# Own part of layers three and four folded into the seven quarter products

## The chip, the cores and the metric

The kernel runs on one core of a Trainium2 chip. The metric is the device time of one execution in microseconds, the median of three runs. All tensors are fp32. TensorE multiplies into PSUM, VectorE (DVE), ScalarE (ACT) and GpSimd (POOL) work on SBUF, and the SyncE queue issues the transfers from and to HBM.

## The reference

There are 16 graphs (batches) of N = 1024 nodes with D = 128 features, each with its own adjacency matrix. Two graph networks follow one another, each with a residual and a layer norm:

```python
def _L0_gnn_ref(embeddings, adjacency_matrix, cost_matrix, W, b):
    degree = adjacency_matrix.sum(axis=-1)[:, :, None]
    sum_neighbors = jnp.einsum('bid,bij->bjd', embeddings, cost_matrix) / degree
    concatenated = jnp.concatenate([embeddings, sum_neighbors], axis=-1)
    return jax.nn.relu(jnp.einsum('bnk,dk->bnd', concatenated, W) + b)

def _layer(nodes, adj, ws, bs, wd, bd, wn, bn, wu, bu):
    src_agg = jnp.einsum('bjv,bij->biv', nodes @ ws + bs, _l2norm(adj, 2))
    dst_agg = jnp.einsum('bjv,bji->biv', nodes @ wd + bd, _l2norm(adj, 1))
    self_rep = nodes @ wn + bn
    upd = jnp.concatenate([src_agg, self_rep, dst_agg], axis=2)
    return jnp.tanh(upd @ wu + bu)
# four layers; inputs: x | layer 1 | layer 2 with layer 1 | layer 3 with layer 1 and x
x = _layernorm(x + _L0_gnn_ref(x, adj, adj, W, b))
x = _layernorm(x + _L1_gnn_ref(x, adj, ...))
```

The layers of the second network take 128, 128, 256 and 384 input features, that is 1, 1, 2 and 3 chunks of 128. `_l2norm` divides adj by the root of the sum of squares of its rows or columns.

## The kernel before, in words

The weights are multiplied through first: in each layer the kernel needs *message weights* (ws and wd times their parts of wu) and *own weights* (wn times its part of wu, the tiles `wown`). Features lie transposed, 128 features on the partitions and 1024 nodes in the free dimension.

A layer has two stages. `messages` (L595) multiplies features by message weights into PSUM, in four groups of nodes, and DVE adds the bias at L607, which gives the tiles t. Then DVE forms sums of quarters of t: S3 (L619, in two halves), S1 (L620), S2 (L621), S4 (L622). `aggregate` (L655) then adds three parts into the same sums: the messages times adj (DST), the messages times adj transposed (SRC), and the own part, which is own weights times features. For the first two, t and adj are cut in 2 x 2 quarters and multiplied in the Strassen-Winograd way: seven products M1, M2, M3, M4, Z11, Z12, Z21 of quarters and of sums of quarters instead of eight. The sums of adj's quarters are the tiles T2 to T4 and Q2 to Q4 (`combined`, `combine_1` and `combine`, L577 to L591). The results are put together afterwards by ACT copies and DVE additions (L685 to L715), and `squash` applies tanh.

Each product makes 64 rows, half of the 128 columns of the array. So the lists `upper` and `lower` name two streams of matmuls, one for each half of the array, and the loop at L765 issues one of each in turn: one step. `events` puts the reads of finished products, and `hooks` other work, ahead of a step of a given number. In before the own part stands first in both lists: for each chunk and each half of the nodes one matmul above and one below, so 2, 2, 4 and 6 steps in layers one to four. Every layer besides has 28 steps for messages (14 in each of DST and SRC). Batch 0 does its layer one in `plain_layer` (L625).

Every engine works its own list in the written order (`manual_schedule`, L794). What belongs to the next batch is hooked into the stages of the present one: in layer three the scaling of the next adj by its column norms (L345, after the transfer of cinv) and its first quarter sums, then directly `first_gnn` of the next batch (L470, records m_f and z_f, with L452, L461, L467 and L498 to L518 on DVE), and in layer four its layer norm: sum (L361), centring (L368), squares (L377, hook 0, the name v), then after a small matmul (pv) the line L385 (ve), a power on GpSimd (L387), and the scaling L392 (y). After that come the transposed features x1 (L427), T2 (L587) and T3 (L589), transposes of rows (L564), the end of the layer (L694, L711, L698, L702, L703, L775), and the next batch's layer one: L607, S3 and so on, more transposes, T4 (L591), and Q2 (L587) to Q4.

Message weights are kept in HBM (`wsave`) and loaded before each layer into one buffer, tag "wm" (`message_weights`, L172). Own weights stay in SBUF for the whole run (L99).

Of the kernel before, what the change touches and what calls it, by code (L numbers as in the profile page):

```python
# [23 lines left out]
def adj_resnorm_kernel(ctx: ExitStack, tc: tile.TileContext, x, adj, w0, b0, layers, out):  # L24
# [67 lines left out]

    ident = const.tile([P, P], F32, name="ident")
    fold = const.tile([P, P], F32, name="fold")
# [3 lines left out]
    b0c = const.tile([P, 1], F32, name="b0c")  # L98
    wown = [const.tile([P, CHUNKS[l], P], F32, name=f"wown{l}") for l in range(NL)]  # L99
    bout = [const.tile([P, 1], F32, name=f"bout{l}") for l in range(NL)]  # L100

    one = ctx.enter_context(tc.tile_pool(name="one", bufs=1))
    two = ctx.enter_context(tc.tile_pool(name="two", bufs=2))
    wsave = [kept_weights.tile([P, CHUNKS[l] + 1, 2 * P], F32, name=f"wsave{l}") for l in range(NL)]

# [19 lines left out]
    def fetch_weights(raw, l, q, wm=None):  # L125
        ws, bs, wd, bd, wn, bn, wu, bu = layers[l]
        nch = CHUNKS[l]
        flat = raw.take(max(3 * nch * P, (nch + 1) * 2 * P))
        wr = flat[:, :3 * nch * P].rearrange("p (k c v) -> p k c v", k=3, c=nch)
        for k, w in enumerate((ws, wd, wn)):  # L130
            q.dma_start(wr[:, k], w.rearrange("(c p) v -> p c v", p=P))
        wur = raw.take(3 * P).rearrange("p (k v) -> p k v", k=3)
        q.dma_start(wur, wu.rearrange("(c p) v -> p c v", p=P))
        bc = raw.take(4)
        for k, v in enumerate((bs, bd, bn, bu)):
            q.dma_start(bc[:, k:k + 1], v.rearrange("(p o) -> p o", o=1))
        if wm is None:
            wm = flat[:, :(nch + 1) * 2 * P].rearrange("p (c v) -> p c v", c=nch + 1)
        return wr, wur, bc, wm, [raw.take(3 * P).rearrange("p (k v) -> p k v", k=3) for _ in range(nch)]
# [21 lines left out]
    def fold_end(l, fetched):  # L161
        _, wur, _, wm, wTs = fetched
        for c in range(CHUNKS[l]):
            pm = small(f"wm{l}_{c}", [HW])
            for k in range(3):
                nc.tensor.matmul(pm[:, k * P:(k + 1) * P], wTs[c][:, k], wur[:, PART[k]],
                                 start=True, stop=True)
            nc.scalar.copy(wm[:, 1 + c], pm[:, :2 * P])
            nc.scalar.copy(wown[l][:, c], pm[:, 2 * P:3 * P])
        nc.sync.dma_start(wsave[l], wm[:, :CHUNKS[l] + 1])  # L170

    def message_weights(b, l):  # L172
        wm = message_tile(f"wm{l + 1}_{b}")
        nc.sync.dma_start(wm[:, :CHUNKS[l] + 1], wsave[l])
        return wm
# [294 lines left out]
    def first_gnn(b, msgs, xT, y, T2, dinv):  # L470
# [38 lines left out]

        events = {4: m1_and_m4_read, 8: m2_read, 10: m3_read}  # L510
        up, lo = flat_steps(upper, high), flat_steps(lower, low)
        for i, pair in enumerate(zip(up, lo)):
            if i in events:
                events[i]()
            for o, x_, y_, start, stop in pair:
                nc.tensor.matmul(o, x_, y_, start=start, stop=stop)  # L516
        nc.vector.tensor_add(e0, e0, Z0)
# [10 lines left out]
    def flat_steps(groups, rows):  # L528

        flat = []  # L530
        for m, (acc, first, mms) in enumerate(groups):
            later = [g[1] for g in groups[m + 1:] if g[0] is acc]
            last = not later or later[0]
            for i, (x_, y_) in enumerate(mms):
                flat.append((acc[rows], x_, y_, first and i == 0, last and i == len(mms) - 1))
        return flat

    def add_x(yT, xT, h):
# [85 lines left out]

    def plain_layer(b, l, feats, t, a, at, fT, etag, hooks):  # L625

        w = wown[l]
        Z = [product(f"z{h}_{l}_{b}", h) for h in range(NH)]  # L630
# [6 lines left out]

        steps = [(Z[h], w[:, c], blocks(f[:, half(h)]), k == 0, False) for h in (1, 0) for k, (f, c) in enumerate(feats)]
        steps += [(Dn[h], x(j, DST), a[:, j, half(h)], k == 0, k == NB - 1) for h in (1, 0) for k, j in enumerate(latter)]
# [14 lines left out]

    def aggregate(b, l, feats, msgs, a, at, T, Q, fT, etag, hooks={}, pieces=1):  # L655


        w = wown[l]
        n = len(feats)
        X, S = msgs  # L660
# [11 lines left out]

        def own(v, h):
            return [(w[:, c, v * V:(v + 1) * V], blocks(f[:, half(h)])) for f, c in feats]

# [25 lines left out]
        def second_half():  # L701
            nc.vector.tensor_add(e2, e2, Z1)  # L702
            nc.vector.tensor_add(e1, e1, e2)  # L703
# [14 lines left out]
        if l == 0:  # L718
# [16 lines left out]

            events = {8: m3_half, 12: m1_read, 20: m4_and_m2_read, 24: last_reads}
        else:

            first_of_lower = [(Ck, True, prod("M4", DST) + prod("M4", SRC)), (Dk, True, prod("M3", DST))]
            reads_of_lower = [m4_read, m3_half]  # L740
            if l < NL - 1:
                first_of_lower.reverse()
                reads_of_lower.reverse()
            upper = [
                (Z1, True, own(1, 1)), (Z0, True, own(1, 0)),
                (A, True, prod("M1", DST) + prod("M1", SRC)), (Bk, True, prod("M2", DST) + prod("M2", SRC)),
                (A, True, prod("M3", SRC)),
                *((Z0, False, prod("Z21", part)) for part in ((SRC, DST) if l == NL - 1 else (DST, SRC))),
            ]
            lower = [  # L750
                (Z1, True, own(0, 1)), (Z0, True, own(0, 0)),
                *first_of_lower,
                (Z1, False, prod("Z12", SRC) + prod("Z12", DST)),
# [3 lines left out]
            def first_reads():  # L757
                m1_read()
                reads_of_lower[0]()

            events = {8: first_reads, 12: reads_of_lower[1], 16: m2_and_half_of_m3, 20: last_reads}

        up, lo = flat_steps(upper, high), flat_steps(lower, low)
        assert len(up) == len(lo)
        for i, pair in enumerate(zip(up, lo)):  # L765
            if i - 2 * n in events:
                events[i - 2 * n]()
            if i in hooks:
                hooks[i]()
            for o, x, y, start, stop in pair:  # L770
                if len(y.shape) == 4:
                    o = nodes(o)
                nc.tensor.matmul(o, x, y, start=start, stop=stop)  # L773
        if pieces == 1:
# [15 lines left out]
    def feature(b, tag):  # L790
        return one.tile([P, N], F32, tag=tag, name=f"{tag}{b}")

    eng = mybir.EngineType
# [201 lines left out]
    for b in range(B):  # L995
# [8 lines left out]
        if b == 0:  # L1004
# [50 lines left out]
            T = combined(0, "T")  # L1055
            plain_layer(b, 0, feats, t, a, at, f1, "acc", hooks)
            wm = message_weights(b, 1)
            a2 = load(n)
            xs2 = load_spread(n)
        else:  # L1060
# [4 lines left out]
            t = messages(b, 0, feats, wm)  # L1065
            wm = message_weights(b, 1)
            Q = combined(b, "Q")

            def rows3():
# [10 lines left out]
            def first_addition(st=st):  # L1080
                if nxt:
                    add_squares(n, st, 1)

            hooks = {0: rows3, 3: lambda: combine(4, y, T), 5: lambda: combine_1(yt), 7: lambda: combine(2, yt, Q),
                     9: lambda: combine(3, yt, Q), 11: lambda: combine(4, yt, Q), 17: sums1, 28: first_addition}
            aggregate(b, 0, feats, t, a, at, T, Q, f1, "row", hooks)
            a2, xs2 = w.get("a"), None

# [3 lines left out]
        t = messages(b, 1, feats, wm)  # L1092
        wm = message_weights(b, 2)

# [18 lines left out]
        else:  # L1113
# [24 lines left out]
            hooks = {0: begin1, 11: centre1, 14: squares1, 18: rstd1, **sums_of_next}  # L1138
        aggregate(b, 1, feats, t, a, at, T, Q, f23, "row", hooks)
        if b:  # L1140
# [61 lines left out]
        t = messages(b, 2, feats, wm, between)  # L1202
        wm = message_weights(b, 3)
        aggregate(b, 2, feats, t, a, at, T, Q, f23, "acc", hooks)
        if nxt:
# [73 lines left out]
        else:  # L1279
            x1v = one.tile([P, HW], F32, tag="x", name="x1_last")  # L1280
            nc.scalar.copy(nodes(x1v), blocks(x1T[:, half(0)]))

            def residual_last():
                o = nodes(f4[:, half(1)])
                nc.vector.tensor_add(o, o, blocks(x1T[:, half(1)]))

            def transpose_last():
                pn["last"] = ps_t.tile([P, BPH, P], F32, tag="pt", name="on_1")
                for q in range(BPH):
                    i = BPH + q  # L1290
                    nc.tensor.transpose(pn["last"][:, q], f4[:, i * P:(i + 1) * P], ident)
                stats[1] = norm_stats(pn["last"], range(BPH), f"1_{b}_1", True)
# [3 lines left out]
        if nxt:  # L1296
            wm = message_weights(n, 0)
            T[4] = one.tile([P, NJ, HW], F32, tag="T4", name=f"T4_{b}_again")
        aggregate(b, 3, feats, t, a, at, T, Q, f4, "row", hooks, 1 if nxt else 2)
        if nxt:  # L1300
# [12 lines left out]
    for i in pieces:  # L1313
        pn[i] = ps_t.tile([P, 2, P], F32, tag="pt", name=f"on_0_{i}")
        for q in range(2):
            nc.tensor.matmul(pn[i][:, q], x1v[:, (i + q) * P:(i + q + 1) * P], ident, start=q == 0, stop=False)
    for q in range(BPH):
# [3 lines left out]
    for i in pieces:  # L1321
        for q in range(2):
            nc.tensor.matmul(pn[i][:, q], f4[:, (i + q) * P:(i + q + 1) * P], ident, start=False, stop=q == 1)
        stats[i] = norm_stats(pn[i], range(2), f"1_{b}_0_{i}")
# [33 lines left out]
```

## Time and profile before

| | |
|---|---|
| time, median of 3 (lowest to highest) | 2424.94 us (2424.76 to 2425.18) |
| span of the profiled execution | 2421.9 us |
| granted TensorE clock | full in nearly the whole span |
| layer three, `aggregate`, batch 3: 563.41 to 591.00 | TensorE 27.59 us busy, DVE 24.38 |
| layer four, batch 3: 616.81 to 646.22 | TensorE 29.41, DVE 22.31 |
| layer one, batch 4: 649.68 to 675.44 | TensorE 25.76, DVE 23.98 |
| layer two, batch 4: 678.93 to 705.00 | TensorE 26.07, DVE 22.62 |

A line of the timeline gives the start, the duration, the engine, the line of the kernel, the operation, what is written from what, the shape, and how many neighbours of one kind were joined; brackets tell the engine's idle time before it and who ended it. A line of the groups gives the same for all instructions of a kind, with busy time and the mean of one in ns. PEld is the loading of weights into the array, which goes on beside the matmuls. The ends of matmuls are modelled, so that durations of TensorE overlap; their starts are what counts.

### The profile page before, as it was taken

To read this page: it belongs to the slowest core of one execution; us is meant where nothing else is said; L and a number is where in the kernel's file an instruction comes from. 1 tells how busy PE (TensorE), PEld (TensorE's weight loads), DVE (VectorE), ACT (ScalarE), POOL (GpSimd) and SP (SyncE) were. 2 spreads that over 40 slices of the span, in tenths; PEclk is the share of its full clock that TensorE was granted. 3 is DMA by queue.
4 is the path that set the end of the run, shared out by engine and by line. 5 is a ranking of instruction groups with operands and counts; after the bars stand their busy time and mean duration, and the time that the engine had idled before them with its cause. 6 is when DMAs were issued, how large, how long until landed. Compare 5 with 4: busy or idle time off the path is not lost.

```text
span 2421.9 us, 34377 instructions
## 1 busy us (share of the span) xinstructions
PE 2407.9 (99%) x13245; PEld 955.6 (39%) x13245; DVE 1904.8 (79%) x2495; ACT 958.5 (40%) x1794; POOL 273.5 (11%) x100
## 2 busy tenths in 40 slices
PE   8999999999999999999999999999999999999998
PEld 5433343333433343333433434334333343333433
DVE  5878878798787978879788787887878878797743
ACT  5425334262442624435143352533425334262321
POOL 4100111101111011110011110111100111101100
PEclk9999999999999999999999999999999999999999
DMA  9517254261633517235172442725427264361410
GB/s 210 116 47 148 49 125 87 68 126 44 144 73 81 109 45 163 62 83 107 49 153 60 90 100 65 143 53 109 88 67 141 46 129 87 68 123 44 97 25 9
DMA packets 365731, 219.92 MB, mean 91 GB/s; under 512 B 152768, under 2 KB 336832, under 8 KB 365568
## 3 DMA queue, kind: packets, MB, share of 16 engines
q1 hardware_dynamic: 364800, 215.36, 42.0%
q0 software_dynamic: 768, 2.36, 0.3%
q8 instruction: 105, 1.72, 0.3%
q14 instruction: 58, 0.48, 0.1%
HBM read 199.17 MB, written 18.46 MB: 90 GB/s over the span
## 4 chain that ended last, share of the span: by engine, by line
PE 97%; DMA 1%; SPq 1%; DVE 0%; ACT 0%; issue 0%; POOLq 0%; DVEq 0%
PE m L773 44%; PE z L773 26%; PE pt L183 16%; PE m_f L516 5%; PE pw L183 2%; PE z_f L516 2%; DMA raw<-in_L_gnn_ws_dram 1%; PE z L652 1%; ACT Q L556 0%; SPq L549 0%; PE d L652 0%; DMA wsave<-wm 0%; DMA a<-in_adj_dram 0%; DMA raw<-in_L_gnn_wn_dram 0%; PE pv L183 0%
## 5 line engine op out<-in xcount | busy, mean ns | idle before, releaser
L773 PE MATMUL m<-Q,S 128*64 128x512 f32 x1008 | 444.9, 593 | 0.0
L387 POOL TENSOR_TENSOR rs<-ve,mhalf 128x32 f32<-128x32 f32 x30 | 191.6, 6385 | 1941.5 <-DVE ve L385 1941.5
L773 PE MATMUL m<-T,S 128*64 128x512 f32 x1008 | 394.9, 593 | 0.0
L773 PE MATMUL m<-at,t 128*64 128x512 f32 x1008 | 394.2, 593 | 0.0
L773 PE MATMUL m<-a,t 128*64 128x512 f32 x1008 | 391.7, 593 | 0.0
L607 DVE TENSOR_TENSOR t<-pt,wm 128x512 f32<-128x512 f32 x256 | 173.3, 686 | 138.4 <-PE pt L183 138.4
L773 PEld LDWEIGHTS m<-Q,S 128*64 128x64 f32 x1008 | 135.6, 137 | 280.1 <-issue 270.0
L686 ACT COPY e<-m 64x512 f32<-64x512 f32 x63 | 36.7, 582 | 501.8 <-PE m L773 501.4
L773 PE MATMUL z<-a,S 128*64 128x512 f32 x504 | 227.0, 593 | 0.0
L773 PE MATMUL z<-a,t 128*64 128x512 f32 x504 | 226.8, 592 | 0.0
L773 PE MATMUL z<-at,S 128*64 128x512 f32 x504 | 226.7, 592 | 0.0
L773 PE MATMUL z<-at,t 128*64 128x512 f32 x504 | 226.6, 592 | 0.0
L773 PE MATMUL z<-Q,t 128*64 128x512 f32 x504 | 226.6, 592 | 0.0
L183 PE MATMUL pt<-wm,f1T 128*64 128x256 f32 x1536 | 213.3, 381 | 0.0
L345 DVE TENSOR_TENSOR a<-a,cinv 128x512 f32<-128x512 f32 x250 | 154.3, 694 | 27.8 <-DMA cinv<-dr 22.3
L773 PEld LDWEIGHTS m<-T,S 128*64 128x64 f32 x1008 | 120.1, 137 | 137.1 <-issue 135.3
L773 PE MATMUL z<-T,t 128*64 128x512 f32 x384 | 172.8, 592 | 0.0
L773 PEld LDWEIGHTS m<-at,t 128*64 128x64 f32 x1008 | 117.9, 137 | 135.9 <-issue 131.6
L773 PEld LDWEIGHTS m<-a,t 128*64 128x64 f32 x1008 | 119.1, 137 | 129.6 <-issue 126.2
L183 PE MATMUL pt<-wm,f23T 128*64 128x256 f32 x1024 | 154.1, 379 | 0.0
L253 ACT ACTIVATE sq<-a 128x1024 f32<-128x1024 f32 x120 | 125.8, 1049 | 69.1 <-DVE acc L262 63.0
L183 PE MATMUL pt<-wm,x_T 128*64 128x256 f32 x1024 | 135.5, 379 | 0.0
(238 smaller groups left out, 4196.9 us busy)
## 6 DMA issues: line engine op xcount, KB each, us to landing
a<-in_adj_dram SPq DMA_DIRECT2D x120, 512.0 KB, 11.2
a<-in_adj_dram SPq DMA_DIRECT2D x240, 128.0 KB, 4.3
rows<-in_adj_dram SPq DMA_DIRECT2D x240, 64.0 KB, 3.0
wm<-wsave SPq DMA_DIRECT2D x16, 512.0 KB, 4.7
xn<-in_x_dram SPq DMA_DIRECT2D x124, 64.0 KB, 1.9
wm<-wsave SPq DMA_DIRECT2D x31, 256.0 KB, 3.9
xs<-in_x_dram SPq DMA_DIRECT2D x60, 128.0 KB, 3.6
cinv<-dr SPq DMA_DIRECT2D x30, 256.0 KB, 5.2
```

Source lines behind the costliest of these rows:

```text
L183: nc.tensor.matmul(out[s], x[:, s], y, start=start, stop=stop)
L253: nc.scalar.activation(sq, a[:, i, :], AF.Square, accum_out=state["cols"][:, i:i + 1])
L345: engine.tensor_mul(a[:, i, s], a[:, i, s], cinv[:, s])
L387: nc.gpsimd.tensor_tensor(rstd, ve, mhalf[:, :n], ALU.pow)
L516: nc.tensor.matmul(o, x_, y_, start=start, stop=stop)
L607: nc.vector.tensor_add(t[j][:, o:o + 2].rearrange("p k a v c -> p k (a v c)"), pt, wm[:, 0][:, None, :].to_broadcast([P, 2, 2 * P]))
L652: nc.tensor.matmul(nodes(o) if len(y.shape) == 4 else o, x_, y, start=start, stop=stop)
L686: nc.scalar.copy(e0[high], A[high])
L773: nc.tensor.matmul(o, x, y, start=start, stop=stop)
```

## The change

The own part of layers three and four is a product as well: own weights (128 outputs, 256 inputs) times features (256 inputs, 1024 nodes). With two chunks taken together it can be cut into quarters like the messages, and then its own seven products can be added into the sums of M1 to Z21 directly, as one more row of each. Layer three has just two chunks; in layer four two of its three are paired and the third (`rest`) stays as it was. This is meant to spare matmuls of TensorE.

For it the weights need quarter sums (`own_sums`, four small DVE operations once a layer, at the start) and the features need them in each batch (`feature_sums`, four DVE operations of 128 x 512, written over the features, in layer three partly into a buffer of tag "wm"). M3 is made in both halves of the array, a part in each; its own row is cut in two pieces of 256 nodes, so the two lists are no longer in step: `in_turn` orders the matmuls by the columns issued so far. Wider changes follow: the order of the products in layers three and four, and the numbers of events; own weights of layers one and two lie in the message tile and are loaded with it (so that tile's load for the next layer moves to a hook, 3 in layers one and two, 23 in layer three); the identity lies in the buffer of e0 and is made again for the end of the last batch.

```diff
+    PAIRED = {2: (1, 0), 3: (1, 2)}
+    wx = {l: const.tile([P, REST + (CHUNKS[l] - 2) * P], F32, name=f"wx{l}") for l in PAIRED}
+    ident = one.tile([P, HW], F32, tag="e0", name="ident")[:, :P]
...
+    def own_sums(l):
+        def w(at):
+            return wx[l][:, at:at + V]
+        nc.vector.tensor_sub(w(S3W), w(0), w(S1W))
+        nc.vector.tensor_add(w(S1W), w(S1W), w(P + V))
+        nc.vector.tensor_sub(w(S2W), w(S1W), w(0))
+        nc.vector.tensor_sub(w(S4W), w(P), w(S2W))
...
+    def in_turn(up, lo):
+        order, at = [], 0
+        for i, step in enumerate(up):
+            order.append((at, 0, i, step))
+            at += step[-1]
+        end, at = at, 0
+        for step in lo:
+            order.append((at, 1, None, step))
+            at += step[-1]
+        assert at == end
+        for _, _, i, step in sorted(order, key=lambda v: v[:2]):
+            yield i, step[:-1]
...
+            y4, y3 = (y[0, 1], y[0, 0]) if sums is None else sums
+            def feature_sums():
+                nc.vector.tensor_sub(y4, y[0, 1], y[0, 0])
+                nc.vector.tensor_sub(y[1, 1], y[1, 1], y4)
+                nc.vector.tensor_sub(y3, y[1, 1], y[0, 0])
+                nc.vector.tensor_sub(y[1, 0], y[1, 0], y[1, 1])
...
+            own_of = {"M1": (w(0), y[0, 0]), "M2": (w(S2W), y[1, 1]), "M3": (w(S3W), y3), "M4": (w(S1W), y4),
+                      "Z11": (w(P), y[1, 0]), "Z12": (w(S4W), y[1, 1]), "Z21": (w(P + V), y[1, 0])}
...
+            lower_m3 = of_own("M3", slice(0, G // 2)) + m3[NJ - 1:]
+            upper_m3 = m3s[:NJ - 1] + of_own("M3", slice(G // 2, G)) + m3s[NJ - 1:]
...
+            if l < NL - 1:
+                upper = [
+                    (A, True, of_own("M1") + prod("M1", DST) + prod("M1", SRC)),
+                    (Bk, True, prod("M2", DST) + prod("M2", SRC) + of_own("M2")), (A, True, upper_m3),
+                    (Z0, True, prod("Z21", DST) + prod("Z21", SRC) + of_own("Z21")),
+                ]
+                lower = [
+                    (Z1, True, of_own("Z12")), (Z0, True, of_own("Z11") + z11[:2]), (Dk, True, m3[:NJ - 1]),
+                    (Ck, True, m4), (Dk, False, lower_m3), (Z1, False, z12), (Z0, False, z11[2:]),
+                ]
+                events = {2: feature_sums, 9: m1_read, 16: m4_read, 18: m3_half_and_m2_read, 23: m3_read, 26: second_half}
+            else:
+                upper = [
+                    (Z1, True, own(1, 1, rest)), (Z0, True, own(1, 0, rest)),
+                    (A, True, of_own("M1") + prod("M1", DST) + prod("M1", SRC)),
+                    (Z0, False, of_own("Z21")),
+                    (Bk, True, of_own("M2") + prod("M2", DST) + prod("M2", SRC)), (A, True, upper_m3),
+                    (Z0, False, prod("Z21", SRC) + prod("Z21", DST)),
+                ]
+                lower = [
+                    (Z1, True, own(0, 1, rest)), (Z0, True, own(0, 0, rest)),
+                    (Z1, False, of_own("Z12")), (Z0, False, of_own("Z11")),
+                    (Ck, True, m4), (Dk, True, m3[:NJ - 1] + lower_m3),
+                    (Z1, False, z12), (Z0, False, prod("Z11", SRC) + prod("Z11", DST)),
+                ]
+                events = {4: feature_sums, 11: m1_read, 13: m4_read, 17: m3_half, 21: m2_and_half_of_m3, 26: last_reads}
...
+        sums = message_tile(f"fs_{b}").rearrange("p c v -> p (c v)")
+        hooks = alongside(hooks, {23: weights3})
-        aggregate(b, 2, feats, t, a, at, T, Q, f23, "acc", hooks)
+        aggregate(b, 2, feats, t, wm, a, at, T, Q, f23, "acc", hooks, sums=(sums[:, half(0)], sums[:, half(1)]))
```

In layer four hooks at the same number as an event come after it; `feature_sums` is event 4 there, `squares0` (L377) hook 0 and `rstd0` (L385 and L387) hook 7. In layer three `feature_sums` is event 2 and the next batch's hooks are 2 (L312), 4, 5, 7 and 9 (L345) and later.

## The prediction

> **What bounds the kernel now.** I read the shares of the engines first, then the groups by shape, the waits, and the timeline of batch 3 and the start of batch 4.
>
> ```profile
> PE 2407.9 (99%) x13245; PEld 955.6 (39%) x13245; DVE 1904.8 (79%) x2495; ACT 958.5 (40%) x1794; POOL 273.5 (11%) x100
> ...
> L773 PE MATMUL z<-f1T,wown 128*64 128x512 f32 x384 | 96.0, 592 | 0.0
> ...
> L183 PE MATMUL pt<-wm,f1T 128*64 128x256 f32 x1536 | 213.3, 381 | 0.0
> ```
>
> TensorE is never idle for long; VectorE (DVE) fills 79%. Each matmul of the program leaves two records, and two column halves run at once. In the timeline, pairs of 512-wide records start 0.43 us apart (664.27, 664.70, 665.13), so one step (an upper and a lower matmul of 512 columns) takes 2 x 0.427 = 0.855 us, 0.858 for the own part, and 256-wide ones half of that (four records in 0.43 us). The period of one batch is 148.5 us (L619 of layer one stands at 502.09 and again at 650.62), almost all of it such steps. But an average hides where DVE sets the pace. The layer-four stage of batch 3 runs from 616.9 to 646.2, then come the messages and layer one of the next batch:
>
> ```profile
> 621.61 1.21 DVE L377 TENSOR_REDUCE v<-sq 128x32 f32<-128x1024 f32 x1
> 623.24 0.19 DVE L385 TENSOR_SCALAR ve<-pv 128x32 f32<-128x32 f32 x1 [0.42 <-PE pv L183]
> 623.34 2.28 DVE L591 TENSOR_TENSOR T_again<-a,T 128x2048 f32<-128x2048 f32 x1
> 630.94 1.23 DVE L392 TENSOR_TENSOR y<-y,rs 128x1024 f32<-128x1024 f32 x1 [5.32 <-POOL inv L240]
> ...
> 647.01 0.65 DVE L775 TENSOR_TENSOR e<-e,z 128x512 f32<-128x512 f32 x1
> 647.59 1.28 DVE L607 TENSOR_TENSOR t<-pt,wm 128x512 f32<-128x512 f32 x2
> 649.03 0.69 DVE L607 TENSOR_TENSOR t<-pt,wm 128x512 f32<-128x512 f32 x1 [0.17 <-PE pt L183]
> 649.89 0.69 DVE L607 TENSOR_TENSOR t<-pt,wm 128x512 f32<-128x512 f32 x1 [0.17 <-PE pt L183]
> 650.62 0.76 DVE L619 TENSOR_TENSOR S<-t 128x256 f32<-128x256 f32 x2
> ```
>
> The numbers in brackets are DVE's idle time before the line. From 630.94 on there is next to none: one wait of 0.68 us for a copy of ScalarE, then 0.17 twice. From 650.62 to 665.03 there is none at all. And at the end of that run TensorE takes its operand as it is written:
>
> ```profile
> 662.74 2.29 DVE L587 TENSOR_TENSOR Q<-at 128x2048 f32<-128x2048 f32 x1
> ...
> 665.08 0.13 PEld L773 LDWEIGHTS m<-Q,S 128*64 128x64 f32 x1 [0.67 <-DVE Q L587]
> 665.09 0.13 PEld L773 LDWEIGHTS m<-at,t 128*64 128x64 f32 x1
> 665.13 0.60 PE L773 MATMUL m<-Q,S 128*64 128x512 f32 x1
> ```
>
> Q2 (L587) ends at 665.03, its weight load starts 0.05 us later, its matmul another 0.04 us later and 0.42 us after the one before it, so on its beat. The load had waited 0.67 us. Hence a DVE chain from L385 of layer four to Q2 of the next layer one meets TensorE with only some 0.02 us to spare, in every batch.
>
> [...] L392 waits 5.32 us for the power on GpSimd (L387, 7.34 us from 623.57) and nothing written after it moves ahead. So a sum put before L385 delays all that follows. [...] no stretch of before has the two column halves out of step, as the change makes them.
>
> **The change, part by part.** *Removed on TensorE.* The own part of layer three goes from 8 half-array matmuls (4 steps) to seven products, 3.5 steps; layer four from 6 steps to 2 + 3.5. That is 0.5 x 0.858 = 0.43 us for each layer and batch: 32 x 0.43 = 13.7 us at most.
>
> *Halves out of step.* The two 256-wide halves of M3 lie at different places, so the halves of the array run half a matmul apart for 5.5 steps in layer three and 8.5 in layer four. Not shown in the trace: between no cost (independent halves) and a whole slot of 0.43 us for each lone half, 2 x 0.43 a layer against the ideal 0.43 for the two together, which eats the gain. I take no cost, and keep 0.43 us a layer for the range.
>
> *Added on DVE.* Four chained operations (feature_sums) of 128x512 in each of the two layers. The nearest rows are L620 to L622 of the same shape and also chained: 0.69 us each, starts 0.725 apart. 32 x 4 x 0.69 = 88 us of DVE, hidden or not by place:
>
> In layer three they stand after L622 and before L312. For batches 1 to 14 DVE then waits 2.02 us for the DMA of cinv, which takes most of the 2.9; the scaling at L345 starts some 0.7 us later. That is worked off before L498 of the next batch's first network (first_gnn, which follows layer three directly), which sat idle 1.40 us. I cost it at nothing. The M1 product now needs the third message addition (done 563.89) at 564.27 and the fourth (564.48) at 565.98: met. TensorE gains its 0.43 us. In batch 0 the stage after it is already DVE-bound (the weights of x and e take 4.62 us there instead of 3.43): no gain.
>
> In layer four they stand between L377 and L385. Start 622.75, then 3 x 0.725 and one 0.61 to the next independent operation: L385 starts at 625.54 instead of 623.24, 2.30 us later (2.9 less the 0.42 that it waited for pv and the overlaps). Behind L385 stand the power on GpSimd, 7.34 us, and L392, which waits for it; the idle 5.32 us stays, since it follows L385. L392, the x1 transposes, T2, T3, the transposes of rows 2 and 3, and L775 all come 2.30 later. The four L607 then find their inputs ready and run 0.64 apart, from 649.89: the fourth at 651.81 instead of 649.89, S3 at 652.54 instead of 650.62. So 1.92 us remain. TensorE, 0.43 us early, stands at the first M3 of layer one at 650.97 and waits for S3 until about 653.04 (2.07 us); 16 steps later it wants Q2, at 666.73, and gets it at 665.03 + 1.92 + 0.08 = 667.03 (0.30 us more). Against 665.13 before that is 1.90 us later. The 0.43 us of layer four is used up in this wait.
>
> *Moved.* Own weights of layers one and two ride with the message weights: 64 KB more in each of 31 loads. The load for layer two landed at 673.35, needed at 675.4; it may come 2.3 + 0.3 later while its need comes 1.9 later: still met. The load for layer four now starts at hook 23 of layer three, and layer one of the next batch lies between. The four small own_sums fall into the start of batch 0, where DVE had idle stretches of 1.31 and 2.96 us. The identity in e0's buffer, and the copies of x1 and the second identity in the last batch, stand beside 10 us of layer-four messages on TensorE. Cost: nothing.
>
> *Sum.* Fifteen passages from layer four to the next batch at +1.90 = +28.5; layer three in batches 1 to 14, 14 x -0.43 = -6.0; batch 15, without a next one, both layers, -0.86. Together +21.6 on 2424.94: **2446.5 us**, forecast 2446.
>
> **The rivals.** *A: the sums hide, TensorE counts.* For it: TensorE is 99% busy and DVE has 20% idle, 5.32 us of it in this very stage. Then 31 x 0.43 = 13.3 us come off (batch 0's layer three gains nothing): 2411.6. Against: the idle time lies behind L385, which the sums precede, and Q2 has no slack. *B: the delay of DVE is half of what I take*, because some of the run from L392 to Q2 has slack that the line view does not show: 15 x 0.95 - 6.9 = +7, 2432; if it only balances the gain, no change. *C: as forecast, but lone halves cost their slot.* In layer four this drowns in the wait for S3; in layer three the gain goes, +6: 2453; another 0.43 a layer on top would make 2459. For it: no row shows it either way.
>
> **How the numbers follow.** Forecast 0.66, C 0.17, B 0.08 (a third of it within 0.2%), A 0.09. The range leaves out A and the low half of B, and C's worst end: 2435 to 2456. Faster by over 0.2%: A, 0.09. Within 0.2%: 0.03. Slower: 0.88.
>
> **What would show it.** Right: L385 starts about 2.3 us later, counted from the end of layer four's messages; TensorE shows a gap near 2 us before the first M3 of layer one in batches 1 to 15, a smaller one before Q2, and none in layers two to four; layer three lasts 27.15 us instead of 27.58. DVE near 1993 us busy. Wrong: layer one still lasts 25.76 us (then A), or layer three does not get shorter (then C). What would upset all: a longer wait for weights at 675, or DVE late enough in layer three to hold first_gnn.

## The result and the profile after

The changed kernel takes 2453.23 us (median of 4 runs, 2452.36 to 2454.01) against 2425.06 us for the kernel before beside it: ratio 1.0115, 95% interval 1.01 to 1.0129. The forecast was 2446, range 2435 to 2456.

The first lines of the page of the changed kernel; line numbers have moved (L607 is now L648, L385 L408, L392 L415, L587 L628, L773 L856, L183 L206):

```profile
PE 2418.3 (99%) x13245; PEld 1032.5 (42%) x13245; DVE 1988.7 (81%) x2631; ACT 957.9 (39%) x1795; POOL 274.0 (11%) x102
...
L856 PE MATMUL m<-a,t 128*64 128x512 f32 x1008 | 415.0, 595 | 9.4 <-DVE t L648 9.4
```

DVE has its 84 us more (1904.8 to 1988.7), and a group that hardly waited before, the first products of layer one (M1, m<-a,t), now stands behind L648, the message additions. The timeline of VectorE at the passage from batch 3 to batch 4 shows why (start, length, idle before the line in brackets); batch 3's layer four starts at 624.79, batch 4's layer one at 657.14:

```profile
629.50 1.21 DVE L400 TENSOR_REDUCE v<-sq 128x32 f32<-128x1024 f32 x1
630.63 0.68 DVE L798 TENSOR_TENSOR f1T<-f1T 128x512 f32<-128x512 f32 x1
...
632.75 0.69 DVE L801 TENSOR_TENSOR x_T<-x_T 128x512 f32<-128x512 f32 x1
633.35 0.18 DVE L408 TENSOR_SCALAR ve<-pv 128x32 f32<-128x32 f32 x1
633.46 2.28 DVE L632 TENSOR_TENSOR T_again<-a,T 128x2048 f32<-128x2048 f32 x1
641.05 1.23 DVE L415 TENSOR_TENSOR y<-y,rs 128x1024 f32<-128x1024 f32 x1 [5.32 <-POOL inv L263]
...
657.77 2.47 DVE L648 TENSOR_TENSOR t<-pt,wm 128x512 f32<-128x512 f32 x4
...
660.28 0.76 DVE L660 TENSOR_TENSOR S<-t 128x256 f32<-128x256 f32 x2
```

L408 starts 8.56 us after the start of layer four; L385 before, 6.35 (623.24 less 616.89): 2.21 later. The four sums have used up the 0.42 that L385 waited for pv, and the 5.32 of idle stay where they were, behind it. The four L648 now run without the two waits of 0.17, and S3 (L660) comes at 35.49 after the start of layer four instead of 33.73. It is so in all 15 batches, within 0.01 us. TensorE at the same place:

```profile
657.14 1.93 PE L856 MATMUL z<-x_T,wm 128*64 128x512 f32 x8
659.70 1.07 PE L856 MATMUL m<-a,t 128*64 128x512 f32 x2 [0.63 <-DVE t L648]
660.85 0.61 PE L856 MATMUL m<-T,S 128*64 128x512 f32 x1
...
674.94 0.64 PE L856 MATMUL m<-Q,S 128*64 128x512 f32 x1 [0.17 <-DVE Q L628]
```

The first of M3 (m<-T,S) comes 3.71 us after the start of layer one, where it came 1.72 after before (651.40 less 649.68): 1.98 us late, and 0.15 after the first half of S3 ends (660.70). From there to the first product with Q2 it is 14.09 us instead of 13.73: 0.36 more. The wait that the trace names, 0.63 us for L648, is that of M1 in the other half of the array, which needs the third message addition (it ends at 659.65) and comes before M3.

From the first matmul of each stage to that of the next, batch by batch, the 28.9 us between the two spans (2421.9 and 2450.8) are made up so:

| where | us |
|---|---|
| layer one, 15 passages: 25.76 became 27.96 to 28.39 in thirteen, 29.39 and 30.09 in two | +38.1 |
| layer three 27.583 to 27.157 (16 times), layer four 29.330 to 28.903 (15 times) | -13.2 |
| layer four of the last batch, with the end of the kernel | -0.2 |
| batch 0, before its first message: the first loads landed later | +1.4 |
| batch 0, from its first message, through layer one, to the products of layer two: 48.31 to 51.82 | +3.5 |
| batch 0, layer two, TensorE's clock at half for 3.41 us | +0.7 |
| batch 0, messages of layer three, and the first network of batch 1 behind it | -1.4 |

The +1.4 us before the first message is put down to chance. That message starts at 35.35 us in the profile of before, and at 35.99 to 38.05 in all others, also in the one run below whose start is that of the kernel before (36.08).

The 3.5 us are the small sums of own weights, as an experiment below shows. (The texts recorded there call this stretch the one to layer one; the messages that wait at its end are those of layer two.) The timeline of VectorE and GpSimd at the start of batch 0 of the changed kernel:

```profile
55.03 0.23 DVE L122 TENSOR_TENSOR wx<-wx 128x64 f32<-128x64 f32 x1 [3.41 <-ACT wx L190]
...
63.56 1.29 DVE L122 TENSOR_TENSOR wx<-wx 128x64 f32<-128x64 f32 x1
...
67.34 1.19 DVE L125 TENSOR_TENSOR wx<-wx 128x64 f32<-128x64 f32 x1
...
63.49 4.96 POOL L368 TENSOR_TENSOR a<-a,cinv 128x512 f32<-128x512 f32 x4 [1.00 <-PE d L690]
```

Layer three's four wait for the copies of the folded weights (3.41 us, where the column scalings of the kernel before stood after 1.3) and hold the scalings back. Layer four's run beside four multiplications on GpSimd and take 1.13 to 1.29 us each, where layer three's, with nothing running on GpSimd, took 0.22 to 0.23: about one GpSimd operation (4.96 / 4 = 1.24) to each. In the end TensorE waits 2.54 us for its features, and its granted clock drops to 0.50 from 86.63 to 90.04. (A line of such windows gives the stretch, its length, the busy time and the number of instructions of PE, PEld, DVE, ACT and POOL, then the granted clock, the busy share of the DMA engines and GB/s.)

```profile
85.85 2.96 PE L206 MATMUL pt<-wm,f1T 128*64 128x256 f32 x16 [2.54 <-ACT f1T L869]
```
```profile
82.00:86.00 4.00, 1.46 (x16) 0.73 (x12) 4.00 (x5) 0.93 (x2) 0.00 (x0) 1.00 1.03 207
86.00:89.50 3.50, 3.50 (x20) 1.77 (x20) 1.58 (x3) 3.50 (x7) 0.00 (x0) 0.59 1.27 164
```

### The profile page after: what moved, and what is told of

Same layout as the page of the kernel before. It is cut to its first block, busy times and chain, and to the rows that moved or that the text cites. A ratio compares the mean times of both kernels' runs of the same rounds, so it can differ in the third digit from the quotient of the medians.

```text
span 2450.8 us, 34735 instructions
## 1 busy us (share of the span) xinstructions
PE 2418.3 (99%) x13245; PEld 1032.5 (42%) x13245; DVE 1988.7 (81%) x2631; ACT 957.9 (39%) x1795; POOL 274.0 (11%) x102
## 3 DMA queue, kind: packets, MB, share of 16 engines
q8 instruction: 105, 1.72, 0.3%
## 4 chain that ended last, share of the span: by engine, by line
PE 80%; DVE 9%; DMA 5%; issue 2%; POOL 2%; SPq 1%; ACT 1%; DVEq 0%; POOLq 0%; ACTq 0%
PE m L856 37%; PE z L856 18%; PE pt L206 15%; PE m_f L537 5%; PE z_f L537 2%; PE pw L206 2%; DMA a<-in_adj_dram 2%; POOL rs L410 2%; DVE at L605 2%; DMA rows_acc<-in_adj_dram 1%; SPq L590 1%; DVE at L624 1%; DVE Q L628 1%; DVE T L632 1%; DVE T L628 1%
## 5 line engine op out<-in xcount | busy, mean ns | idle before, releaser
L856 PE MATMUL m<-Q,S 128*64 128x512 f32 x1008 | 453.2, 593 | 1.5 <-DVE Q L628 1.2
L856 PE MATMUL m<-a,t 128*64 128x512 f32 x1008 | 415.0, 595 | 9.4 <-DVE t L648 9.4
L856 PE MATMUL m<-at,t 128*64 128x512 f32 x1008 | 411.3, 595 | 2.7 <-DVE at L605 2.7
L856 PE MATMUL m<-T,S 128*64 128x512 f32 x1008 | 394.8, 593 | 1.2
L648 DVE TENSOR_TENSOR t<-pt,wm 128x512 f32<-128x512 f32 x256 | 170.5, 684 | 135.1 <-PE pt L206 135.1
L856 PEld LDWEIGHTS m<-Q,S 128*64 128x64 f32 x1008 | 135.6, 137 | 256.3 <-issue 237.0
L856 PE MATMUL z<-at,t 128*64 128x512 f32 x504 | 229.2, 592 | 0.0
L856 PE MATMUL z<-a,S 128*64 128x512 f32 x504 | 227.3, 594 | 0.0
L856 PE MATMUL z<-a,t 128*64 128x512 f32 x504 | 226.8, 592 | 0.0
L856 PE MATMUL z<-at,S 128*64 128x512 f32 x504 | 226.7, 592 | 0.0
L856 PE MATMUL z<-Q,t 128*64 128x512 f32 x504 | 226.6, 592 | 0.0
L206 PE MATMUL pt<-wm,f1T 128*64 128x256 f32 x1536 | 214.3, 382 | 2.5 <-ACT f1T L869 2.5
L856 PEld LDWEIGHTS m<-a,t 128*64 128x64 f32 x1008 | 124.2, 137 | 158.2 <-issue 124.4
L856 PEld LDWEIGHTS m<-T,S 128*64 128x64 f32 x1008 | 123.1, 137 | 128.0 <-issue 124.6
L856 PEld LDWEIGHTS m<-at,t 128*64 128x64 f32 x1008 | 124.9, 137 | 123.8 <-issue 109.5
L856 PE MATMUL z<-T,t 128*64 128x512 f32 x384 | 172.8, 592 | 0.0
L206 PE MATMUL pt<-wm,f23T 128*64 128x256 f32 x1024 | 154.0, 379 | 0.0
L206 PE MATMUL pt<-wm,x_T 128*64 128x256 f32 x1024 | 136.1, 379 | 0.0
```

What stands on the lines that cost most here:

```text
L206: nc.tensor.matmul(out[s], x[:, s], y, start=start, stop=stop)
L648: nc.vector.tensor_add(t[j][:, o:o + 2].rearrange("p k a v c -> p k (a v c)"), pt, wm[:, 0][:, None, :].to_broadcast([P, 2, 2 * P]))
L856: nc.tensor.matmul(o, x, y_, start=start, stop=stop)
```

## The experiments

Twelve kernels in three groups, each with runs of the kernel before on the same chip (medians 2426.06, 2425.00 and 2426.08 us). Below, "+" and "-" are against that; the changed kernel stands at +28.2. Some of the kernels leave sums out, or let products read summed features that should read raw ones, as is said with each. These compute other values than the change, and only say where time goes; the shapes of their operations stay the same.

**Layer four without its sums.**

```diff
-                events = {4: feature_sums, 11: m1_read, ...
+                events = {11: m1_read, ...
```

> The changed kernel with layer four's four feature sums left out (its own products then read the raw features); nothing else differs. Theory D (the sums hold back VectorE ahead of the epsilon addition at L408, and with it the chain that ends at S3 and Q2 of the next layer one): layer one falls back to 25.76 us in batches 1 to 14 from 27.96 to 29.39; the last batch keeps its 30.09, because there a row load waits in its queue; 2453.2 - 33.6 = about 2419.6 us. Rival T (the lost time sits on TensorE: weight loads, column halves out of step, the new order of products): layer one keeps 28 us and the time stays near 2453. A value half way, near 2436, would mean that both have a share.

Measured: 2424.12 us (2421.85 to 2426.86), -1.9, ratio 0.9991 (0.9983 to 1.0). Without the sums 30.1 us come off: rival T falls. But it is 3.6 us short of the forecast. Layer one lasts 25.79 to 26.26 us in twelve of the batches 1 to 14, 27.8 in two, 31.1 in the last. In those two (batches 4 and 6) VectorE waits for the last loaded rows:

```profile
657.30 1.26 DVE L605 STREAM_TRANSPOSE at<-rows_xa 128x512 f32<-128x512 f32 x2
660.44 1.30 DVE L605 STREAM_TRANSPOSE at<-rows_acc 128x512 f32<-128x512 f32 x2 [1.88 <-ACT rows_acc L597]
```

TensorE is here 0.43 us earlier and VectorE is not. So layer four's gain runs into Q2 and into those rows; it is not enough to hide the sums, VectorE has to come earlier as well.

**The sums behind L408.** The power on GpSimd keeps VectorE idle for 5.32 us; the sums fit there if the products that read them come later. The first two versions put Z11 and Z12 of the own part behind the sums too, where they read summed features in place of raw ones, so that their arithmetic is not that of the change, unlike what the first recorded text says; the third has the list of the changed kernel there. The third:

```diff
-                    (Z0, False, of_own("Z21")),
-                    (Bk, True, of_own("M2") + prod("M2", DST) + prod("M2", SRC)), (A, True, upper_m3),
+                    (Bk, True, of_own("M2")), (Z0, False, of_own("Z21")),
+                    (Bk, False, prod("M2", DST) + prod("M2", SRC)), (A, True, upper_m3),
...
-                events = {4: feature_sums, ...
+                events = {8: feature_sums, ...
...
-            hooks = {0: squares0, 7: rstd0, 10: rows0, ...
+            hooks = {0: squares0, 7: rstd0, 9: again, 10: rows0, ...     # again: T_again, taken out of rstd0
```

> Layer four's feature sums put behind L408, before T_again; the own products that read them, and the hooks behind, stand later. Same arithmetic. Theory D: they fall into the 5.32 us that VectorE waits for the power on GpSimd, 4 x 0.72 = 2.9 us of it; layer one back at 25.76 us, about 2419.6 us (the last batch keeps its late row load). Rival P (the sums, with two operands in SBUF, hold off the power on GpSimd, as T_again seems to): the power then ends later by up to 2.9 us, L415 as late as in the changed kernel, and the time stays near 2453. If instead the power gets in after the first sum and ahead of T_again, L415 comes up to 1.5 us earlier than before the change and nothing else shows.

> As the kernel with layer four's sums behind L408, but the quarter sums of the next batch are formed two steps later too, behind the last product that reads the old ones (in the first version the last part of layer four's M3 read quarter sums of the next batch). Theory D: the same time as the first version, 2418.7 us within 1.5; layer one at 25.80 us in batches 1 to 14. Rival: the later hook delays VectorE and layer one grows again; each 0.1 us of that in every batch is 1.5 us.

> The changed kernel's own arithmetic, with layer four's sums behind L408 and ahead of T_again, and with the lower half's list left as the change has it (Z11 and Z12 of the own part ahead of the sums, on the raw features, where the two versions before read summed ones). Theory D: the lists of TensorE hardly matter, layer one at 25.80 us in batches 1 to 14, the last batch at 30.5, 2418 us. Rival: with the lower list as it was, the own product of M4 or Z21 meets the sums late, and layer four grows by 0.4 us or more: 2424.

Measured: 2418.70 (-7.4), 2418.13 (-6.9) and 2419.41 us (-6.7; ratio 0.9973, 0.9963 to 0.9984). In all three layer one is 25.79 to 25.80 us in batches 1 to 14 but for one batch each in the last two (26.2 and 25.9). What the second text says of M3 was mistaken; the two versions differed in nothing that shows. VectorE and GpSimd in layer four of batch 3 of the third, and GpSimd in the changed kernel:

```profile
624.43 0.19 DVE L408 TENSOR_SCALAR ve<-pv 128x32 f32<-128x32 f32 x1 [0.45 <-PE pv L206]
624.54 0.68 DVE L798 TENSOR_TENSOR f1T<-f1T 128x512 f32<-128x512 f32 x1
...
627.19 2.28 DVE L632 TENSOR_TENSOR T_again<-a,T 128x2048 f32<-128x2048 f32 x1
630.54 1.23 DVE L415 TENSOR_TENSOR y<-y,rs 128x1024 f32<-128x1024 f32 x1 [1.07 <-POOL inv L263]
...
624.77 5.74 POOL L410 TENSOR_TENSOR rs<-ve,mhalf 128x32 f32<-128x32 f32 x1 [62.29 <-DVE ve L408]
```
```profile
633.68 7.34 POOL L410 TENSOR_TENSOR rs<-ve,mhalf 128x32 f32<-128x32 f32 x1 [64.47 <-DVE ve L408]
```

The sums cost nothing here, and more is won: the power takes 5.74 us instead of 7.34. Counted from the end of the VectorE operation that is under way when it is issued, it takes the same time in both: 5.28 us behind T_again, 5.29 behind the first sum. So it seems to wait for that one operation, 2.28 us long or 0.68. L415 therefore comes 6.11 us after L408, where it came 7.70 after. Rival P falls, its last sentence was right, and VectorE is early enough for the 0.43 us to be kept.

**Four more operations in the kernel before.**

```diff
+            if l == NL - 1 and hooks and i == 4:
+                g = [f[:, half(h)] for f, _ in feats[:2] for h in range(NH)]
+                nc.vector.tensor_sub(e0, g[1], g[0])
+                nc.vector.tensor_sub(e0, g[3], e0)
+                nc.vector.tensor_sub(e0, e0, g[0])
+                nc.vector.tensor_sub(e0, g[2], e0)
```

> The kernel before, with four more chained subtractions of 128x512 on VectorE at the place where the change puts layer four's sums; their result is not used, TensorE's work is untouched. Theory D: VectorE is 2.3 us later at the epsilon addition, 1.8 to 1.9 of it left at S3 (two short waits absorb the rest), and layer one lasts 1.77 (from the changed kernel: 2.20 less the 0.43 that TensorE was ahead) to 1.90 us longer in 15 batches: 2425.1 + 26.6 to 28.5 = 2451.7 to 2453.6. Rival T (the change's cost is on TensorE): 2425 to 2428. Rival half (half of the delay is absorbed): 2439.

Measured: 2456.90 us, +30.8 (ratio 1.0127, 1.0113 to 1.0141). Four operations at this place in VectorE's queue bring the whole cost of the passages, without any of the change on TensorE: S3 comes 35.48 us after the start of layer four, as in the changed kernel (35.49). Layer one grows by 1.75 to 2.17 us in thirteen passages and by 3.3 and 4.0 in two, again with the wait for the rows (gaps of 1.7 and 2.0 us ahead of m<-at,t).

**Eight operations ahead of L408.**

```diff
                 nc.vector.tensor_sub(y[1, 0], y[1, 0], y[1, 1])
+                if l == NL - 1 and pieces == 1:
+                    nc.vector.tensor_sub(e0, y[0, 1], y4 if sums else y[0, 0])
+                    nc.vector.tensor_sub(e0, y[1, 1], e0)
+                    nc.vector.tensor_sub(e0, e0, y[0, 0])
+                    nc.vector.tensor_sub(e0, y[1, 0], e0)
```

> The changed kernel with four more chained subtractions of 128x512 behind layer four's sums, still ahead of L408, their result not used. Theory D, with no slack left: each of them costs its start-to-start 0.72 us in every one of 15 batches: 15 x 2.9 = 43.5 us more, 2496.7 us, layer one at 30.9 to 31.1 us. Rival half: if some of the path from L415 to S3 and Q2 is free, 20 to 22 us more, 2474.

Measured: 2502.72 us, +77.7, that is 49.5 more than the changed kernel; 43.5 was expected. No slack is left: in all 15 batches S3 comes 2.77 us later than in the changed kernel (38.27 after the start of layer four), which makes 41.6 us. Most of the other 0.5 us of a batch lies in the messages of layer two. TensorE's waits (us in all, times, longest) and the window behind one of them:

```profile
PE z L861 <- DVE e L863: 36.4, 15, 2.4
PE m L861 <- DVE t L648: 10.5, 15, 0.7
```
```profile
211.50:215.00 3.50, 3.01 (x9) 1.30 (x9) 3.39 (x7) 3.50 (x9) 0.00 (x0) 0.57 1.03 235
```

The wait of 2.4 us now lies in the own part of layer one, and in each of the 15 passages the clock is granted at half for 3.41 us after it. From there on one half of the array runs 0.13 to 0.16 us behind the other in twelve passages, and in these the messages of layer two take 4.03 to 4.07 us in place of 3.49. Whether the half clock or the lag between the halves is the cause was not tested.

**Layer three without its sums.**

```diff
-                events = {2: feature_sums, 9: m1_read, ...
+                events = {9: m1_read, ...
```

> The changed kernel with layer three's four feature sums left out (its own products read the raw features). Theory: in layer three they are hidden in the wait for cinv and in the slack of the first network, so nothing changes beyond 1 us: 2452 to 2454; layer three 27.16 us as before. Rival: VectorE's delay there reaches the next stage; then up to 0.7 us a batch, 10 us, would come off: 2443.

Measured: 2454.41 us, +28.3. In layer three the sums are hidden, with little to spare: between batches 3 and 4 the waits that hid them went from 2.02 us (cinv) and 1.40 (ahead of the first network's additions) in the kernel before to none and 0.29 in the changed one.

**The small sums of own weights.** First moved to layers two and three of batch 0, then to two idle places inside its start:

```diff
-        if l in PAIRED:
-            own_sums(l)
...
                 columns0(range(NJ, NB), 1)
+                own_sums(2)
                 destination(1, cinv[0])
...
                 combine_1(y)
+                own_sums(3)
                 finish(1)
```

> Only the eight small sums of own weights are moved, from the start of batch 0 (behind the copies of the folded weights) to layers two and three of batch 0, where GpSimd stands still. Theory O (in the changed kernel they held VectorE from 52.9 to 55.0 us and again from 63.6 to 68.5 us, and the second half of layer one's messages waited 2.54 us for that): the stretch from the first message to layer one of batch 0 falls from 51.8 to 48.3 us; 3.5 us less in all, 4.2 if the dip of TensorE's clock after that wait goes too: 2449 to 2449.7. Rival L (the start is late because the first loads landed 1.2 us later in that profile, and the rest is chance): no change beyond 0.5 us, about 2453.

> The changed kernel with only the eight own sums of weights moved inside the start of batch 0, to two places where VectorE stood idle in the kernel before (behind the first column scalings, and behind the first quarter sum). Theory O: 3.5 us of the stretch before layer one of batch 0 and the 0.73 us of TensorE's clock at half rate come off, and unlike in the run that moved them to layers two and three nothing is given back: 2449.0 us. Rival: they cost as much there: 2453.

Measured: 2450.82 us (+24.8) and 2452.12 us (+26.0, runs from 2450.2 to 2454.5). In both profiles the stretch is 48.3 us again and the clock stays full; in the eight profiles with the sums at the place of the change it is 50.85 to 52.48. So theory O holds for the start. The first gives 1.01 us back in the messages of layer three of batch 0 and 0.83 in the weights behind its first network. The second gives nothing back in batch 0; but in its profile single batches wait up to 1.6 us longer in layer one than in that of the changed kernel, so that the 4.2 us do not show in the median.

**The rows of the last batch.**

```diff
-                ahead["wm"] = message_weights(b, 1)
+                if nxt:
+                    ahead["wm"] = message_weights(b, 1)
...
-            wm = ahead["wm"]
+            wm = ahead["wm"] if nxt else message_weights(b, 1, nc.gpsimd)
```

> The changed kernel with one edit: in the last batch the message weights of layer two are loaded over GpSimd's queue, so that the loads of the last rows (rows_acc) no longer stand behind them in the queue. Theory W: there the weights wait until layer one's own products have read the old ones, and the rows wait behind; without that the last batch's layer one falls from 30.09 to about 28 us, like the others: 2.1 us less in all, 2451. Rival: the rows are late for another cause (their buffer) and nothing changes.

Measured: 2448.41 us, +23.4, and in the profile the last batch's layer one falls from 30.09 to 27.95. The rest of the difference (4.8 in the medians) lies elsewhere and is put down to chance: the clock's dip in batch 0 is missing in its profile, and the scattered waits of layer one are shorter. In the changed kernel ScalarE waits there for rows that stand behind the weights in the queue:

```profile
2317.07 1.26 DVE L605 STREAM_TRANSPOSE at<-rows_xa 128x512 f32<-128x512 f32 x2
2320.35 1.31 DVE L605 STREAM_TRANSPOSE at<-rows_acc 128x512 f32<-128x512 f32 x2 [2.02 <-ACT rows_acc L597]
...
2318.61 1.70 ACT L597 ACTIVATE rows_acc<-rows_acc,rinv 128x256 f32<-128x256 f32 x4 [5.93 <-DMA rows_acc<-in_adj_dram]
```

**The three edits together**, first with the sums as in the earlier versions, then as in the third:

> Three edits on the changed kernel: layer four's sums behind L408 (as in the run before this one), the own sums of weights in two places of batch 0 where VectorE stood idle (behind the first column scalings, and behind the first quarter sum while it waits for TensorE), and in the last batch the message weights of layer two on GpSimd's queue instead of in front of the row loads. Theory: 2418.7 from the first edit; the stretch from first messages to layer one of batch 0 falls from 50.9 to 48.3 (-2.6), the last batch's layer one from 30.5 to 25.8 (-4.7): 2411.4 us, 14 below the kernel before, that is about the 32 x 0.43 = 13.7 that TensorE was to gain. Rival: VectorE binds somewhere else in batch 0 and gives 1 to 2 us back: 2413.

> The three edits together, with the sums placed as in the run before this one: 2411 us, 14 below the kernel before; layer one at 25.79 us in all 15 batches, layers three and four at 27.16 and 28.90, the first messages of batch 0 to its layer one in 48.3 us. Rival as for that run: layer four longer, 2417.

Measured: 2411.07 us (-13.9; with Z11 and Z12 on summed features) and **2410.51 us** (2410.46 to 2411.32), -15.6, ratio 0.9937 (0.9925 to 0.995). The second has the changed kernel's arithmetic, and is faster than both kernels. The first line of its page, then its timeline at the start of batch 0 and where batch 4 begins:

```profile
PE 2393.7 (99%) x13245; PEld 1032.4 (43%) x13245; DVE 1993.0 (83%) x2631; ACT 957.0 (40%) x1795; POOL 250.7 (10%) x103
```
```profile
54.71 0.22 DVE L122 TENSOR_TENSOR wx<-wx 128x64 f32<-128x64 f32 x1
...
643.64 0.69 DVE L646 TENSOR_TENSOR t<-pt,wm 128x512 f32<-128x512 f32 x1 [0.17 <-PE pt L204]
```

The four sums of own weights (L122) take 0.22 us each in their idle place. VectorE waits for TensorE again in the messages of layer one, layer one lasts 25.80 us in all passages but one (25.94), layers three and four 27.157 and 28.903, and one period 147.71 us instead of 148.525: the two times 0.427, less 0.03.

## Why the prediction was right, point by point

- *Removed on TensorE, 0.43 us a layer*: right to 0.01 us in both layers.
- *Halves out of step cost nothing*: right, with 27.157 us for 27.583 in layer three; that they cost nothing was an estimate, as no stretch of the kernel before has the halves out of step. With a price, rival C's case, layer three could not have got shorter. That the time, 2453, is rival C's number is chance.
- *Layer four's sums ahead of L385*: right. L385 2.30 us later (2.21 measured), 1.92 left at S3 (1.76, since the four message additions follow each other at 0.60 us and not at 0.64), TensorE 2.07 behind at the first M3 (1.98) and 0.30 at Q2 (0.36, in other batches 0.2). After layer four's gain of 0.43 one passage cost 1.77 to 1.96 in ten batches, 2.08 to 2.20 in three; 1.90 was forecast. The term of 28.5 us came to 38.1 - 15 x 0.427 = 31.7 all the same, since two passages cost 3.2 and 3.9: the same delay also made the rows of the next batch late, as their loads stand in the queue behind a load whose buffer VectorE's transposes set free. By the trace the last of them landed 4.7 to 5.4 us after the start of layer one before and 7.6 to 9.0 after (batches 2 to 14). In the last batch, the moved weights stood in front of them (2.1 us). The prediction followed VectorE's delay to TensorE and not to the loads.
- *Layer three's sums hidden*: right, shown by leaving them out. The scaling starts 0.6 us later between batches 3 and 4 (0.7 forecast).
- *Batch 0's layer three gains nothing*: wrong by 1.6 us in the good sense; it gained its 0.43, and the weights in the first network behind it, 4.62 us before, took 3.43. The wait of its column scalings for cinv was 0.24 us where it had been 5.10. The four sums fill part of it, and the transfers come earlier: counted from the start of layer three, the small one (dr) that cinv needs landed at 3.08 us instead of 4.57, and cinv at 8.57 instead of 10.65. Before, the load of layer four's weights stood just ahead of it in the queue, at 0.94; in the changed kernel that load has to wait for the sums, which lie in its buffer. In the run without layer three's sums it stands at 0.94 again, dr lands at 4.59, and this gain of the first network is gone (17.0 us instead of 15.45).
- *Moved: the four small own_sums fall into the start of batch 0, where DVE had idle stretches; cost nothing*: this failed. It cost 3.5 us and 0.7 of clock. The idle stretches were there, 1.31 and 2.96 us, and the run of all three edits uses them; but the sums were written down behind the copies they need, ahead of work that was ready, and in layer four's case beside GpSimd's operations, at 1.2 us each in place of 0.23.
- *Rivals*: A (all hidden, 2411.6) was wrong for this kernel; it is what the kernel with three edits does, at 2410.5. B fell with the four operations in the kernel before (+30.8).

So the sum of 21.6 us became 28.2 (28.9 in the profiles): 3.2 in the passages, 4.2 in the sums of weights, 1.4 of chance at the start and 0.2 that the last layer four fell short, less 1.8 that batch 0 gained. The mechanism and the largest term were right. The result is 7 us off mostly because VectorE's delay was not followed to the loads and because own_sums were put at nothing.

## What to carry to other kernels

Engine time that looks free in a stage is free only behind the instruction that the idle time waits for: 2.9 us of VectorE cost 30 us over 15 batches ahead of a power on GpSimd and nothing just behind it. Before saving matmuls, ask whether the engine that feeds TensorE has slack as well, and follow a delay to buffers and queued loads, not only to the next operand. One-time work at the start is in the queue too: look at what stands behind it, and what runs on GpSimd beside it.

## What the runs showed of the hardware

- Two column halves of the array half a matmul out of step lost nothing here: layer three takes 27.157 us where it took 27.583, 0.43 less in every batch. The offset is one of a matmul's two records, so the records of the halves still start within 0.01 us of each other there. A lone 256-wide piece of M3 (m<-fs,wx) takes 0.43 us in its half, beside one record of the other half:

```profile
589.88 0.38 PE L856 MATMUL m<-fs,wx 128*64 128x256 f32 x1
589.88 0.59 PE L856 MATMUL z<-at,S 128*64 128x512 f32 x1
590.09 0.38 PE L856 MATMUL m<-fs,wx 128*64 128x256 f32 x1
590.31 0.59 PE L856 MATMUL m<-Q,S 128*64 128x512 f32 x1
590.32 0.59 PE L856 MATMUL z<-a,S 128*64 128x512 f32 x1
```

- The power on GpSimd over 128x32 ended 5.28 us after the VectorE operation under way when it was issued in the changed kernel (T_again), and 5.29 after it in the third version (the first sum). Once begun it did not hold VectorE back: in the third version three sums and T_again run beside it at 0.68 to 0.69 and 2.28 us.
- TensorE's clock went to half for 3.41 us after some of its waits. Matmul starts 2.9 us apart in batch 0 were followed by it in four of eight profiles (in the changed kernel 2.92, to 85.85), 3.0 in the steady part in all of 15 passages of the run with eight operations (0.57 granted in the window above), 3.4 to 4.1 in the last batch in all of four profiles (without layer four's sums 4.06, to 2294.30, where the next records take 1.06 to 1.11 us and not 0.59). In the changed kernel neither 2.27 (to 2321.12) nor, at its very start, 2.73 (to 13.26) was, with 1.00 granted after both.
